# A two-layer GRU and a mixture of experts on one core: other places for small operations in five steps, and for two parts of the shared expert

## The chip, the core and the metric

The kernel runs on one of the eight cores of a Trainium2 chip. The metric is the device time of one execution in microseconds (us), as a median over several executions. A core has TensorE (PE, matrix products; PEld is its loading of weights), VectorE (DVE), ScalarE (ACT), GpSimd (POOL) and SyncE (SP). The first four compute; SP, ACT and POOL issue DMAs. [...]

## The reference

Two blocks with a residual around each. x is 2 x 1024 x 256, all in float32.

```
x = x + gru_block(x, cond)            # first block
x = x + moe_block(x, cond)            # second block

gru_block:  mixed = tanh(x @ W_in.T + b_in + cond)
            h1 = gru(mixed, layer 0);  h2 = gru(h1, layer 1)
            gate = sigmoid(cond @ W_gate.T + b_gate)
            return (gate * h2 + h2) @ W_out.T + b_out
  gru step: r, z = sigmoid(...);  n = tanh(xn + r * hn);  h = (1 - z) * n + z * h

moe_block:  shared = (silu(x @ w1) * (x @ w3)) @ w2          # 256 -> 512 -> 256
            s = sigmoid([x, cond] @ router_W)                # 8 experts
            the two best of s + bias; their s, normalised, are the shares
            routed = sum of share * (gelu(x @ W1e[e]) @ W2e[e])
            return (shared + routed) / 3
```

The recurrence runs over 1024 steps. The second block has 2048 tokens.

## The kernel before

**The recurrence in chunks.** The 1024 steps of a row are cut into 16 chunks of 62 steps (the first 32 steps are run once, in the run-up of the chunk that follows them). All chunks of both rows run side by side, as 32 columns of a state. A chunk does not know the state that it should begin with, so each layer first runs through the chunk before it (`AHEAD`: 62 steps for layer 0, 44 for layer 1), and takes the end as the beginning of the next (`go_round`). Whether the guess fits is measured at the end (`fit`), and a slow exact path exists for the case that it doesn't; it is not executed here, and its instructions follow a branch at the end.

**Ticks.** One loop runs over 126 ticks. In a tick layer 0 does one step and layer 1 does the step of two ticks earlier (`LAG`). `position(layer, tick)` is zero where the counted run of a layer begins: tick 62 for layer 0, tick 64 for layer 1. Layer 1 runs from tick 20 on. For each layer of a tick, `finish_scanned` issues: the sigmoid of both gates (ACT, L341), a scan for the sum inside tanh (DVE, L344), the tanh (ACT, L355), a product with the old state's row (DVE, L357), a scan that gives the new row (DVE, L360), and a transpose to the state that TensorE takes next (DVE, L369). TensorE then multiplies the state (`add_state`, L296) and the input of the next layer (`feed`, L268). VectorE takes the layers in turn.

The order is written out by hand: a scheduler is switched off for the loop (`manual_schedule`), and other work is put into named places of a tick: `place(tick, where, what)`, with "product" (TensorE, behind layer 0's state product), "behind" (TensorE, behind layer 1's), "n0" (before layer 0's tanh), "scan0" and "scan1" (on VectorE, between the product with the old row and the row's scan of layer 0 or 1) and "end". `plan` places the first block's output product for finished groups of tokens there; `front.prepare` places the gate of the first block: a product (`gate_sums`), its sigmoid, and what follows.

Three kinds of operation stand at the beginning of single steps. In the step at position -33 the state of the run-up that begins at step 0 must become zero: `keep` makes a masked row (`kept`, L337). At position 0 the state `begin` is turned back to rows by a transpose (`turned`, L484), called at the head of the tick. At tick 54 the gates' product stands in "product".

**The tail.** After the last tick `front.all_of` does the last group: its output product, the residual, the logits of the router (`route`, `keep_logits`) and the transposes to token rows. The results go to `given` in memory. The first part of the shared expert's hidden layer is begun in the last ticks (`begin_hidden`).

**The second block** (`moe`). Here a scheduler that knows the engines orders the instructions. There are 16 parts of the shared hidden layer (4 blocks of 512 tokens times 4 slices of 128); a part is four products of 512 columns (`hidden_sums`, L969), a sigmoid (L981), a silu (L982) and a product (L983). The routing is a chain of small VectorE operations from `raw` (L1083) to `pick` (L1179). After it, POOL gathers 128 tokens at a time for the experts (`fetch`, L1274), 35 blocks go through `go_through`, and their results go to `back`. `EARLY` parts are computed beside the routing, one (`FILL`) in the last expert blocks, and the rest in the last stage. There the order is again written by hand: POOL gathers the results back (`fetch_back`, L1335), eight at once and then two for every part; `behind` is a copy of one value (L1334) that makes POOL wait for a tile; `add_gone` adds the gathered rows (L1349); then for each of 16 tiles of tokens TensorE multiplies by w2 (L1367), VectorE adds (L1375) and ACT writes the tile out (L1376). The buffers for sigmoid and silu alternate between two.

Of the kernel before, what the change touches and what calls it, by code (L numbers as in the profile page):

```python
# [8 lines left out]
FP = mybir.dt.float32  # L9
# [8 lines left out]
P = 128  # L18
# [51 lines left out]

EARLY = 8
FILL = EARLY + 1
# [13 lines left out]
def gru_moe(ctx, tc, xT, vec, bias, w_in, wih0, whh0, wih1, whh1, w_out, w_gate, router, w1, w3, w2, w1e, w2e, out):  # L86
# [62 lines left out]
    class Steps:  # L149
# [177 lines left out]
        def finish_scanned(self, layer, to, tick, before_n, after_n, between, keep=None):  # L327
# [6 lines left out]
            sums = by_sum(ps)  # L334
            if keep is not None:
                kept = self.edge.tile([P, U], FP, name=f"kept{layer}")
                nc.vector.tensor_scalar(kept, h, keep, -1.0, ALU.mult, ALU.mult)  # L337
                h = kept

# [12 lines left out]

            n = self.step_pool.tile([P, U, 2], FP, name=f"n{layer}")
            before_n()
            nc.scalar.activation(n[:, :, 0], s[:, 1 : 2 * U : 2], AF.Tanh, scale=-1.0 if keep is None else keep)  # L355
# [45 lines left out]
    with ExitStack() as stack:  # L401
        g = Steps(stack, "", on_pe=False, rest_of_x=rest_of_x)
        g.gates = [
            [g.gru_only.tile([P, 2, U, 2], FP, name=f"gates{layer}{i}") for i in range(2)] for layer in range(2)
# [134 lines left out]
        def keep_of(layer, tick):  # L539

            return not_first[:, 0:1] if position(layer, tick) == -FIRST - 1 else None

        def let_wait(ins, copied):
# [52 lines left out]

        places = {}

        def place(tick, where, what):
            places.setdefault((tick, where), []).append(what)  # L600

        def placed(tick, where):
# [40 lines left out]
        place(last_tick - 1, "behind", lambda: begin_hidden("w3", [0]))  # L643
        place(last_tick - 1, "end", silu)
        for block in range(1, N // MB):
            place(block, "end", lambda block=block: spread(block))
# [4 lines left out]
        for i, todo in enumerate(front.prepare(g.bank)):  # L651
            for where, what in todo.items():
                place(AHEAD[0] - 8 + i, where, what)
        def negate_first():
# [31 lines left out]
        with tc.manual_schedule():  # L686
            for tick in range(AHEAD[0] + S + LAG):
                now = [layer for layer in range(2) if runs(layer, tick)]
                for layer in now:
                    if layer not in g.states:  # L690
                        g.states[layer], g.rows[layer] = zero_state, zero_row
                    elif position(layer, tick) == 0:
                        g.starts[layer] = g.states[layer] = begin[layer]
                        g.start_rows[layer] = g.rows[layer] = turned(g.starts[layer], f"start_row{layer}")
                work = work_of(tick)
# [74 lines left out]
    with tc.If(n_fit < P):  # L770
        with ExitStack() as stack:
# [45 lines left out]
            temp = [room[:, NT + i : NT + i + TB // D, :].rearrange("p s d -> p (s d)") for i in (0, TB // D)]  # L817
            front.hidden(0, 0, *(front.hidden_sums(g.bank, 0, 0, name)[0] for name in ("w1", "w3")), *temp)
        moe(tc, "_turn", front, out)


class Front:
# [17 lines left out]
    def prepare(self, bank):  # L840

        nc, vec_sb, later, ps = self.tc.nc, self.vec_sb, self.later, {}

        def gate_sums():
            ps["gate"] = bank("ps_gate")[:, 0 : KD * B].rearrange("p (k b) -> p k b", b=B)
            for m in range(KD):
                for k in range(KD):
                    last = nc.tensor.matmul(
                        out=ps["gate"][:, m, :],
                        lhsT=later["w_gate"][:, k, m * P : (m + 1) * P],  # L850
                        rhs=vec_sb[:, COND + k * B : COND + (k + 1) * B],
                        start=(k == 0),
                        stop=(k == KD - 1),
                    )
            return last
# [135 lines left out]

    def all_of(self, bank, group, between=lambda: None, behind=lambda: None):
        for m in range(KD):
# [5 lines left out]
        self.keep_logits(group)  # L999
        behind()  # L1000
        tiles = range(group * GS * R // P, (group + 1) * GS * R // P)
# [8 lines left out]
def moe(ctx, tc, tag, front, out):  # L1010
# [210 lines left out]

    parts = [(blk, m) for blk in range(N // TB) for m in range(KS)][1:]

# [104 lines left out]
    def fetch_back(behind=None):  # L1328
# [3 lines left out]
        yb = rows[:, AWAY + i % (ROWS - AWAY), :]  # L1332
        if behind is not None and i % 2 == 0:
            nc.gpsimd.tensor_copy(yb[0:1, 0:1], behind[0:1, 0:1])  # L1334
# [116 lines left out]
```

## Time and profile before

| what | value |
|---|---|
| time, median of 5 executions | 538.44 us (536.91 to 539.21) |
| the profiled execution | 539.21 us, of which the span from first to last instruction 537.5 us |
| PE busy | 512.7 us (95%), 7492 products |
| DVE busy | 385.7 us (72%) |
| ACT busy | 244.1 us (45%) |
| POOL busy | 76.9 us (14%) |
| HBM | 21.26 MB read, 9.57 MB written |
| from the last tick's end to the last instruction | 361 us to 537.5 us |

Lines of a profile are read like this. A group has its source line, engine, operation, what it writes and reads, the shape, a count, and then busy time, the mean of one in ns, and the idle time of the engine just before, with what ended it. A row of the timeline has its start and its length in us, and in brackets the idle time before it and what released it. "issue" means that the profile shows nothing that the engine waited for. TensorE's busy time is modelled: a matmul's end is not measured, and a full row does not mean that it works at its best. The granted clock is the share of TensorE's full clock that its throttle let through. "PE 512.7 (95%)" alone says little: what a change in one stage is worth is read from that stage.

### The profile page before, as it was taken

How to read it: one execution, taken by the hardware profiler on the slowest of the kernel's cores; microseconds unless marked ns; L12 is line 12 of the kernel's file. 1: busy time of each engine (PE TensorE's matmuls, PEld its weight loads, DVE VectorE, ACT ScalarE, POOL GpSimd, SP SyncE). 2: the span in 40 equal slices, each digit the busy share in tenths (PEclk: the TensorE clock that was granted, in tenths of full speed). 3: DMA queues.
4: the chain of work that ended last, by engine and by line, in shares of the span. 5: the costliest groups of instructions: out<-in, count | busy, mean ns of one | idle time of the engine just before them, and what ended most of it. 6: DMA issues, size and time to landing. Idle time of an engine off the chain costs nothing. (4 is left out here: it accounts for less than half of the span.)

```text
span 537.5 us, 18511 instructions
## 1 busy us (share of the span) xinstructions
PE 512.7 (95%) x7492; PEld 341.3 (64%) x7492; DVE 385.7 (72%) x1296; ACT 244.1 (45%) x833; POOL 76.9 (14%) x124
## 2 busy tenths in 40 slices
PE   7999999999999999999999999989999999999795
PEld 4556766676665545566665666654468888844584
DVE  3765699999888888888988888888943333335362
ACT  3444355665566555656566566632133333331000
POOL 1200000000000000000000000002064444037570
PEclk9999999999999999999999999999999999999888
DMA  8980000000000000000000000001034433223252
GB/s 287 372 256 2 2 3 4 3 4 2 4 32 3 12 1 4 2 23 22 4 22 8 17 23 3 22 22 60 1 97 124 124 119 128 70 70 98 88 168 85
DMA packets 23103, 32.13 MB, mean 60 GB/s; under 512 B 3056, under 2 KB 18544, under 8 KB 22992
## 3 DMA queue, kind: packets, MB, share of 16 engines
q1 hardware_dynamic: 17344, 19.94, 10.9%
q0 software_dynamic: 3216, 8.79, 5.8%
q10 hardware_dynamic: 2448, 2.11, 1.2%
q8 instruction: 63, 1.03, 0.8%
q14 instruction: 32, 0.26, 0.2%
HBM read 21.26 MB, written 9.57 MB: 57 GB/s over the span
## 5 line engine op out<-in xcount | busy, mean ns | idle before, releaser
L296 PE MATMUL ps_step<-whh_sb,h 128*32 128x192 f32 x3616 | 193.3, 331 | 5.2 <-DVE h L369 3.8
L296 PEld LDWEIGHTS ps_step<-whh_sb,h 128*32 128x32 f32 x3616 | 94.6, 109 | 71.3 <-DVE h L369 51.4
L360 DVE TENSOR_TENSOR_SCAN row<-gates,n 128x128 f32<-128x128 f32 x230 | 97.7, 425 | 29.6 <-ACT n L355 28.3
L344 DVE TENSOR_TENSOR_SCAN ps_step<-gates,ps_step 128x128 f32<-128x128 f32 x230 | 97.4, 424 | 14.3 <-ACT gates L341 14.2
L268 PE MATMUL ps_step<-wih_sb,h 128*32 128x192 f32 x1696 | 99.7, 328 | 4.1 <-ACT ps_step L526 2.4
L355 ACT ACTIVATE n<-ps_step 128x64 f32<-128x64 f32 x228 | 53.1, 233 | 111.0 <-DVE ps_step L344 110.9
L341 ACT ACTIVATE gates<-ps_step 128x128 f32<-128x128 f32 x230 | 66.8, 290 | 34.8 <-PE ps_step L296 25.7
L268 PEld LDWEIGHTS ps_step<-wih_sb,h 128*32 128x32 f32 x1696 | 57.5, 109 | 26.8 <-ACT ps_step L526 14.2
L369 DVE STREAM_TRANSPOSE h<-row 128x64 f32<-128x64 f32 x230 | 56.5, 246 | 8.1
L969 PE MATMUL ps_w<-x_sb,w_sb 128*128 128x512 f32 x128 | 57.3, 597 | 0.1
L268 PE MATMUL ps_in<-wih_sb,h 128*32 128x192 f32 x1024 | 54.4, 328 | 1.5 <-ACT h L257 1.1
L1239 DVE COPY hT<-ps_hT 128x256 f32<-128x256 f32 x35 | 14.9, 425 | 48.9 <-PE ps_hT L1237 47.1
L526 ACT COPY ps_step<-inputs 128x256 f32<-128x256 f32 x123 | 47.7, 388 | 0.0
L357 DVE SCALAR_TENSOR_TENSOR n<-gates,row 128x64 f32<-128x64 f32 x224 | 47.1, 210 | 0.0
L268 PEld LDWEIGHTS ps_in<-wih_sb,h 128*32 128x32 f32 x1024 | 34.1, 110 | 14.3 <-issue 4.6
L526 ACT COPY ps_step<-bt 128x256 f32<-128x256 f32 x106 | 39.9, 377 | 3.3
L1274 POOL DMA_INDIRECT inputs<-given,pick x35 | 33.3, 951 | 55.2 <-PE ps_xT L1237 31.8
L969 PEld LDWEIGHTS ps_w<-x_sb,w_sb 128*128 128x128 f32 x128 | 23.6, 190 | 27.1 <-issue 24.7
L1245 PE MATMUL ps_h<-w1e_sb,xT 128*128 x140 | 36.1, 380 | 0.7 <-DVE xT L1239 0.7
L1245 PE MATMUL ps_y<-w2e_sb,hT 128*128 x140 | 36.0, 380 | 0.0
L1335 POOL DMA_INDIRECT inputs<-back,slots x32 | 30.7, 959 | 29.8 <-issue 27.5
L1245 PEld LDWEIGHTS ps_y<-w2e_sb,hT 128*128 128x128 f32 x140 | 26.4, 190 | 4.8 <-DVE hT L1239 1.2
(179 smaller groups left out, 432.4 us busy)
## 6 DMA issues: line engine op xcount, KB each, us to landing
back<-y SPq DMA_DIRECT2D x35, 128.0 KB
w1e_sb<-in_w1e SPq DMA_DIRECT2D x1, 2048.0 KB
w2e_sb<-in_w2e SPq DMA_DIRECT2D x1, 2048.0 KB
given<-inputs SPq DMA_DIRECT2D x8, 256.0 KB
out_dram<-inputs ACTq DMA_DIRECT2D x16, 128.0 KB
whh_sb<-in_whh SPq DMA_DIRECT2D x2, 768.0 KB
x_sb<-in_xT SPq DMA_DIRECT2D x3, 512.0 KB
w_sb<-in_w SPq DMA_DIRECT2D x3, 512.0 KB
```

Source lines behind the costliest of these rows:

```text
L268: last = nc.tensor.matmul(out=out[cols(q), :, :], lhsT=given(k), rhs=self.wih[layer][:, k, q * 3 * U : (q + 1) * 3 * U].rearrange("p (g u) ...
L296: nc.tensor.matmul(out=by_sum(self.sums[layer])[cols(q), 0:3, :], lhsT=self.states[layer][:, k, :], rhs=self.whh[layer][:, k, q * 3 * U : ...
L341: nc.scalar.activation(gates[:, :, :, 1], sums[:, 1:3, :], AF.Sigmoid)
L344: nc.vector.tensor_tensor_scan(s, gates[:, 0, :, :].rearrange("p u i -> p (u i)"), ps[:, 0 : 6 * U : 3], 0.0, ALU.mult, ALU.add,)
L355: nc.scalar.activation(n[:, :, 0], s[:, 1 : 2 * U : 2], AF.Tanh, scale=-1.0 if keep is None else keep)
L357: nc.vector.scalar_tensor_tensor(n[:, :, 1], gates[:, 1, :, 1], 1.0, h, ALU.subtract, ALU.mult)
L360: nc.vector.tensor_tensor_scan(row.rearrange("p u i -> p (u i)"), gates[:, 1, :, :].rearrange("p u i -> p (u i)"), n.rearrange("p u i -> p ...
L369: nc.vector.transpose(to, row)
L526: return nc.scalar.copy(by_sum(banks[layer][tick % 2])[:, 0:4, :], g.sum_bias[1] if layer else inputs[:, group_of(0, tick), :, :],)
L969: last = self.tc.nc.tensor.matmul(out=ps, lhsT=self.later[name][:, k, m * P : (m + 1) * P], rhs=self.x1[:, k, blk * TB : (blk + 1) * TB], ...
L1245: nc.tensor.matmul(out=ps, lhsT=of[:, k, :], rhs=weights_sb[:, bass.ds(e * KD + k, 1), :], start=(k == 0), stop=(k == KD - 1),)
L1274: nc.gpsimd.indirect_dma_start(out=xg, out_offset=None, in_=given[:, :], in_offset=bass.IndirectOffsetOnAxis(ap=pick[:, i : i + 1], axis=0),)
```

## The change

Two groups of edits, in one kernel.

The first group shifts parts of the shared hidden layer. `EARLY` goes from 8 to 6 parts. The list of parts in `moe` begins with the third instead of the second, since a second part is computed in the tail: its first product stands between the output product and the routing's logits, and the rest behind the last transposes. The second half of the first part's w3 product moves to the last tick. Layer 1's `fit` moves behind the tail's `all_of`. In the last stage there are seven parts instead of six, and POOL copies a value ahead of every gather, not of every second.

The second group is about single ticks. The masked rows `kept` are made a half tick earlier, in "scan1" of tick 28 and "scan0" of tick 31. The gates' product is halved over two ticks, 53 and 54. The turn back to rows at positions 0 moves from the head of the tick to behind the sums' scan. The tanh keeps its scale from a tile in the masked steps.

```diff
-EARLY = 8
+EARLY = 6
@@ finish_scanned
-            if keep is not None:
-                kept = self.edge.tile([P, U], FP, name=f"kept{layer}")
-                nc.vector.tensor_scalar(kept, h, keep, -1.0, ALU.mult, ALU.mult)
-                h = kept
...
+            if h is self.turned_row.get(layer):
+                nc.vector.transpose(h, self.states[layer])
             before_n()
@@
+        def mask(layer):
+
+            kept = edge.tile([P, U], FP, name=f"kept{layer}")
+            nc.vector.tensor_scalar(kept, g.rows[layer], not_first[:, 0:1], -1.0, ALU.mult, ALU.mult)
+            g.rows[layer] = kept
...
+        place(AHEAD[0] - FIRST - 2, "scan1", lambda: mask(0))
+        place(AHEAD[0] + LAG - FIRST - 1, "scan0", lambda: mask(1))
@@
+        place(last_tick, "behind", lambda: begin_hidden("w3", [1]))
@@ front.prepare
-                place(AHEAD[0] - 8 + i, where, what)
+                place(AHEAD[0] - 9 + i, where, what)
...
-            {"product": gate_sums, "scan1": lambda: spread(0)},
-            {"n0": gates, "scan1": lambda: spread(1)},
+            {"product": lambda: gate_sums(0), "scan1": lambda: spread(0)},
+            {"product": lambda: gate_sums(1), "scan1": lambda: spread(1)},
+            {"n0": gates},
@@ position 0
-                        g.start_rows[layer] = g.rows[layer] = turned(g.starts[layer], f"start_row{layer}")
+                        g.start_rows[layer] = g.rows[layer] = g.turned_row[layer] = edge.tile(
+                            [P, U], FP, name=f"start_row{layer}"
+                        )
@@ the tail
-                    if position(layer, tick) == S - 1:
-                        fits.append(fit(layer))
+                    if layer == 0 and position(0, tick) == S - 1:
+                        fits.append(fit(0))
...
-            front.all_of(
-                g.bank,
-                GROUPS // GS - 1,
-                lambda: begin_hidden("w3", [1]),
-                lambda: nc.vector.tensor_tensor(
-                    front.hid(0, slice(0, TB)), begun["silu"], begun["w3"], ALU.mult
-                ),
+            nc.vector.tensor_tensor(front.hid(0, slice(0, TB)), begun["silu"], begun["w3"], ALU.mult)
+
+            def begin_next():
+                begun["next"], _ = front.hidden_sums(g.bank, 0, 1, "w1", None, [0])
+
+            front.all_of(g.bank, GROUPS // GS - 1, begin_next)
+            fits.append(fit(1))
+            front.hidden_sums(g.bank, 0, 1, "w1", begun["next"], [1])
+            pb, _ = front.hidden_sums(g.bank, 0, 1, "w3")
+            front.hidden(
+                0,
+                1,
+                begun["next"],
+                pb,
...
@@ moe
-    parts = [(blk, m) for blk in range(N // TB) for m in range(KS)][1:]
+    parts = [(blk, m) for blk in range(N // TB) for m in range(KS)][2:]
@@ fetch_back
-        if behind is not None and i % 2 == 0:
+        if behind is not None:
             nc.gpsimd.tensor_copy(yb[0:1, 0:1], behind[0:1, 0:1])
```

`gate_sums` takes the half `m` as an argument and is otherwise the same; `all_of` loses its argument `behind`; the exact path behind the branch computes two parts instead of one.

More of the change, by code (lines that the diff above doesn't have):

```diff
@@ L402, in gru_moe @@
         g = Steps(stack, "", on_pe=False, rest_of_x=rest_of_x)
+        g.turned_row = {}
         g.gates = [
@@ L541, in keep_of, with place @@
             return not_first[:, 0:1] if position(layer, tick) == -FIRST - 1 else None
+        places = {}
+        def place(tick, where, what):
+            places.setdefault((tick, where), []).append(what)
+        def mask(layer):
[4 more added lines that the diff above has]
+        place(AHEAD[0] + LAG - FIRST - 1, "scan0", lambda: mask(1))
         def let_wait(ins, copied):
@@ L592, in gru_moe @@
         next_rest()
-        places = {}
-        def place(tick, where, what):
-            places.setdefault((tick, where), []).append(what)
         def placed(tick, where):
@@ L744, in gru_moe @@
                 for layer in now:
-                    if position(layer, tick) == S - 1:
-                        fits.append(fit(layer))
+                    if layer == 0 and position(0, tick) == S - 1:
+                        fits.append(fit(0))
             for where in ("n0", "scan0", "end"):
                 placed(AHEAD[0] + S + LAG, where)
-            front.all_of(
-                g.bank,
-                GROUPS // GS - 1,
-                lambda: begin_hidden("w3", [1]),
-                lambda: nc.vector.tensor_tensor(
-                    front.hid(0, slice(0, TB)), begun["silu"], begun["w3"], ALU.mult
-                ),
+            nc.vector.tensor_tensor(front.hid(0, slice(0, TB)), begun["silu"], begun["w3"], ALU.mult)
[10 more added lines that the diff above has]
+                pb,
+                *(g.mixed_pool.tile([P, KD, MB], FP, name="mixed").rearrange("p k n -> p (k n)") for _ in range(2)),
             )
@@ L817, in gru_moe @@
             temp = [room[:, NT + i : NT + i + TB // D, :].rearrange("p s d -> p (s d)") for i in (0, TB // D)]
-            front.hidden(0, 0, *(front.hidden_sums(g.bank, 0, 0, name)[0] for name in ("w1", "w3")), *temp)
+            for m in range(2):
+                front.hidden(0, m, *(front.hidden_sums(g.bank, 0, m, name)[0] for name in ("w1", "w3")), *temp)
         moe(tc, "_turn", front, out)
@@ L842, in prepare, with gate_sums @@
         nc, vec_sb, later, ps = self.tc.nc, self.vec_sb, self.later, {}
[L844 to L854, printed above, removed]
+        def gate_sums(m):
+            if m == 0:
+                ps["gate"] = bank("ps_gate")[:, 0 : KD * B].rearrange("p (k b) -> p k b", b=B)
+            for k in range(KD):
+                last = nc.tensor.matmul(
+                    out=ps["gate"][:, m, :],
+                    lhsT=later["w_gate"][:, k, m * P : (m + 1) * P],
+                    rhs=vec_sb[:, COND + k * B : COND + (k + 1) * B],
+                    start=(k == 0),
+                    stop=(k == KD - 1),
+                )
             return last
@@ L990, in give, with all_of @@
         )
-    def all_of(self, bank, group, between=lambda: None, behind=lambda: None):
+    def all_of(self, bank, group, between=lambda: None):
         for m in range(KD):
@@ L999, in all_of @@
         self.keep_logits(group)
-        behind()
         tiles = range(group * GS * R // P, (group + 1) * GS * R // P)
```

## The prediction

> **What bounds the kernel now.** I read the busy time by stage first, then the chain that ended last, then the timeline around each place that the change touches. The stages (start:end, length; busy time of PE, PEld, DVE, ACT and POOL with counts; granted TensorE clock; DMA share and GB/s):
>
> ```profile
> 361.10:395.20 34.10, 33.22 (x139) 16.05 (x140) 29.36 (x88) 6.65 (x12) 7.68 (x29) 1.00 0.15 47
> 395.20:475.80 80.60, 79.79 (x429) 68.01 (x428) 28.04 (x73) 29.23 (x74) 28.34 (x30) 1.00 0.35 108
> 475.80:496.50 20.70, 20.68 (x49) 9.22 (x50) 11.05 (x19) 3.67 (x6) 14.98 (x19) 1.00 0.32 92
> 496.50:508.30 11.80, 8.00 (x35) 6.11 (x33) 3.14 (x6) 0.60 (x1) 7.07 (x10) 0.95 0.31 90
> 508.30:532.00 23.70, 23.54 (x95) 19.91 (x95) 14.89 (x36) 0.00 (x0) 11.32 (x15) 0.88 0.46 141
> ```
>
> From 361 on TensorE is full in every stage but one: 496.5 to 508.3, where 3.8 us are idle, and where the granted clock falls below 1. The chain says the same of the last 56 us:
>
> ```profile
> 475.82 20.84 PE ps_w L969 x48
> 496.66 6.48 PE ps_s L1367 x30
> ...
> 507.55 0.59 PE ps_s L1367
> 508.14 0.13 issue
> 508.27 23.59 PE ps_s L1367 x95
> 531.88 0.42 DVE inputs L1375
> ```
>
> Six parts of the shared expert (48 instructions in 20.84 us: 0.43 each, 3.43 to 3.47 a part), then 16 rows of output, each 8 instructions at 0.216 us, 1.73 together. From 496.49, 16 times 1.73 would end at 524.2; the last really ends at 531.85. So 7.6 us are lost. What that hole looks like in the timeline:
>
> ```profile
> 487.07 0.18 POOL L1334 COPY inputs<-sig 1x1 f32<-1x1 f32 x1
> 487.28 0.60 ACT L981 ACTIVATE sig<-ps_w 128x512 f32<-128x512 f32 x1 [5.43 <-POOL inputs L1334]
> 499.19 0.60 ACT L981 ACTIVATE sig<-ps_w 128x512 f32<-128x512 f32 x1 [5.95 <-PE ps_s L1367]
> 504.07 0.69 DVE L983 TENSOR_TENSOR inputs<-silu,ps_w 128x512 f32<-128x512 f32 x1 [3.56 <-remote]
> 508.33 0.42 DVE L1375 SCALAR_TENSOR_TENSOR inputs<-ps_s,inputs 128x256 f32<-128x256 f32 x1 [1.74 <-remote]
> ```
>
> Consumers of the sixth part and of output row 0 wait for TensorE until 499.19, 504.07 and 508.33, though its records have those products done at about 495, 497 and 498.6. No row tells what holds it. It falls in the time when POOL issues gathers without a pause (477.36 to 505.65), and ends 2.7 us after it.
>
> **The ticks.** From one transpose of layer 0's state to the next a plain tick takes 2.74 us, and VectorE's chain sets it. The touched ones take 2.95 and 2.93 (masks), 3.14 (gates' product), 3.09 and 3.24 (turns).
>
> ```profile
> 91.80 0.21 DVE L337 TENSOR_SCALAR kept<-row,not_first 128x64 f32<-128x64 f32 x1
> 160.53 1.05 PE L848 MATMUL ps_gate<-vec_sb,w_gate_sb 128*128 128x2 f32 x8
> 162.44 0.29 ACT L341 ACTIVATE gates<-ps_step 128x128 f32<-128x128 f32 x1 [0.48 <-PE ps_step L296]
> 183.56 0.20 DVE L484 STREAM_TRANSPOSE start_row<-begin 128x64 f32<-128x64 f32 x1
> ```
>
> - Masks: each pushes the next scan back by 0.12 (91.80 to 91.93, 98.85 to 98.97); that goes twice. The other 0.09 of those ticks stays: the tanh with its scale from a tile takes 0.32 instead of 0.23. The first mask's new place has 0.18 idle before the scan, as in a plain tick, and two copies of 0.29 together at 163.23 fit in that place without moving the scan (163.50): free. The second comes behind a 0.34 addition (L448) that already fills its place: I charge 0.12. Gain 0.12 (bounds 0 and 0.24).
> - Gates' product: 8 instructions hold TensorE 1.05, layer 1's state product comes late, and the gates wait 0.48; the tick is 0.40 longer. Halves of 0.53 end at 161.06, before layer 1's state is transposed (161.01) and its weights load (some 0.15 later). The nearest row is the context product, as many instructions as a half, in tick 60: the ticks there are 2.74 and 2.73. The half in tick 53 makes the next layer-1 input products move as one block, as in every tick with input work (2.74). Gain 0.40 (0.2 to 0.4). Copies on VectorE move a tick earlier into the same idle place.
> - Turns: they cost 0.12 (183.56 to 183.68) and 0.17 (189.48 to 189.65). In their new place the product with the row must wait for the whole transpose: 0.31 (scan) + 0.23 + 0.21 + 0.03 puts the row scan 0.78 behind the sums' scan, instead of 0.69. Gain 0.29 less 2 times 0.09: 0.11 (0 to 0.29).
>
> Together 0.63 less (0.2 to 0.93), all on the path.
>
> **The tail before routing.** The routing chain on VectorE starts with `raw`:
>
> ```profile
> 365.33 0.29 DVE L1083 TENSOR_TENSOR raw<-logits,context 128x128 f32<-128x128 f32 x1
> 387.83 0.20 DVE L1179 TENSOR_SCALAR pick<-few 128x39 int32<-128x39 f32 x1
> 388.32 1.18 POOL L1274 DMA_INDIRECT inputs<-given,pick x1 [19.99 <-DVE pick L1179]
> 395.19 0.60 PE L1237 MATMUL ps_xT<-ident,inputs 128*128 128x128 f32 x4
> ```
>
> In the changed kernel's order layer 1's fit (8 small operations, 1.2 us) and the whole second part (silu 0.69, product 0.68) stand ahead of `raw` on VectorE. That part's products on TensorE begin behind the last transposes at 365.0: half of w1 0.86, w3 1.72, last end 367.75; then product 0.68 and the count 0.11: `raw` at 368.5, 3.15 later. Fit, sigmoid (0.60) and silu end at 367.4 and are covered. From `raw` to `pick` both orders hold the same: 7 operations of parts on VectorE, 16, 22 and 8 instructions of parts on TensorE. So 22.5 us again, and `pick` at 391.0. Before, the first gather's packets ended at 391.95, the second's at 392.2, and TensorE came for them at 395.19 only, because 18 instructions of parts stood behind the last pick product. Now 2 stand there, done at 391.5. The first two gathers land at 395.1 and 395.35; the experts start at about 395.4. Two parts less in this stage buy nothing: 0.2 later (0 to 0.4). The w3 half that goes behind the last state product (1.02) fits in TensorE's idle 359.9 to 361.1: free; without that idle time it would cost its 1.02. It makes the last two transposed tiles of group 6, their copies on ScalarE and their write on SP (360.56) a microsecond later; they are due at the first gather, 391. On SP the write of zeros to `back` moves behind the read of the count; it is due at 476. Neither costs anything.
>
> **The last stage.** Six parts become seven: 8 times 0.43, 3.43 more on TensorE, on the chain. POOL copies a value before every gather instead of every second: a pair took 2.68 (487.07 to 489.75) and takes 2.82, as each copy's gather takes 1.41. POOL then ends its 32nd gather near 522, landing some 2.3 later; the row that needs it is computed after 526: covered. Each activation and silu of a part reuses the buffer of two parts before and so waits for POOL's copy of it; the last would run at 498.6 and 500.0, before TensorE's seventh part ends (500.2): covered, too, by 0.2.
>
> **Sum.** -0.63 + 0.2 + 3.43 = +3.0, with the hole unchanged. The profiled execution took 539.21 (span 537.5 and 1.7 around it), 0.77 above the median of the five; it would take 542.2, and the median 541.4. Bounds by those above: 540.5 to 542.5 for this case alone.
>
> **Rivals.**
> - *The hole closes* (the other side). One mechanism: if the dense gathers hold TensorE's completions, spacing them by copies frees it: 541.4 - 7.6 = 533.8. For it: the hole ends shortly after the run of gathers. Against: the run stays unbroken. Part 0's sigmoid is there at 477.8 but its copy comes at 487.07, for POOL is 9 us behind and gains 0.6 a part; so gathers go from one per 1.34 to one per 1.41 us. It decides from 3.0 us of the 7.6 on.
> - *The hole shrinks by about half*: 537.5 to 540, near no change. The same rows.
> - *A new idle time halves the clock.* TensorE would now wait from 391.5 to 395.3. In the hole, a gap of 4.6 us with two single matmuls in it was followed by matmuls 0.43 apart instead of 0.216, from 508.3 to 514: 3.0 us. If 3.8 empty us do the same: 544.4. Against: at 360 and 372 gaps of a microsecond did nothing, and nothing between is seen.
> - *The ticks don't shorten*: 542.0; inside the likeliest case's range.
>
> [...]
>
> **Chances.** Likeliest case 0.48 (540 to 543); hole closed 0.26; hole halved 0.12; clock halved 0.14. A difference under 0.3%, 1.6 us, can't be told from none here. Faster: 0.26 and a little of the halved hole, 0.28. Same: most of the halved hole and the lower edge of the likeliest, 0.12. Slower 0.60. The range from 533.5 to 544 leaves out a part of the closed hole and most of the halved clock, some 0.16.
>
> **What would show it.** Ticks 29, 32, 55, 62 and 64 at 2.83, 2.83 or 2.95, 2.74, 3.0 and 3.1. `raw` 3.15 later after the last tick, TensorE idle before the first xT for more than 3 us, 56 instead of 48 instructions of L969 in the last stage. I am wrong if output row 0's addition follows the seventh part's last matmul by 2 us instead of ten (the hole is closed), if `raw` doesn't move, or if TensorE's matmuls are 0.43 apart in the stage of the experts.

## The result, and the profile after

The changed kernel takes 539.22 us (median of 36 runs, 538.07 to 540.62), the kernel before 538.01 (61 runs, 534.71 to 539.33): a ratio of 1.0024, 95% interval 1.0017 to 1.0031. It is slower, as predicted, but by 1.2 us and not by 3.0. The profiled execution took 539.44, its span is 537.7; before it was 539.21 and 537.5.

So small a difference is a sum of large ones. The busy time by stage in the changed kernel (start:end, length; busy time of PE, PEld, DVE, ACT and POOL with counts; granted TensorE clock; DMA share and GB/s):

```profile
360.20:394.60 34.40, 29.15 (x133) 14.01 (x129) 29.08 (x88) 6.51 (x12) 5.79 (x27) 1.00 0.12 39
394.60:402.00 7.40, 6.57 (x20) 4.94 (x21) 2.12 (x5) 0.77 (x2) 5.05 (x6) 0.54 0.36 106
402.00:479.60 77.60, 76.17 (x410) 65.26 (x408) 26.19 (x67) 28.73 (x71) 25.17 (x27) 1.00 0.34 106
479.60:503.70 24.10, 24.10 (x57) 10.72 (x58) 12.20 (x21) 3.58 (x6) 18.93 (x28) 1.00 0.32 92
503.70:512.40 8.70, 8.58 (x40) 7.23 (x38) 3.65 (x7) 0.60 (x1) 5.92 (x10) 1.00 0.33 96
512.40:532.00 19.60, 19.45 (x89) 16.85 (x89) 13.72 (x34) 0.00 (x0) 11.65 (x18) 1.00 0.53 163
```

Two rows answer to the prediction. The experts now begin at a granted clock of 0.54, behind 3.73 us of idle time (`warm` below, with 0.25 us idle and a clock of 1.00, shows that the one makes the other). And from 503.70 on TensorE is full to the end: the hole is gone. The chain that ended last shows the same, with one pause of 0.16 where before 3.8 us lay idle:

```profile
494.85 9.01 PE ps_w L992 x21
503.86 8.42 PE ps_s L1389 x39
512.28 0.16 issue
512.44 19.46 PE ps_s L1389 x89
```

The timeline at the places that matter:

```profile
394.57 0.97 PE L1259 MATMUL ps_xT<-ident,inputs 128*128 128x128 f32 x4 [3.73 <-DMA inputs<-given,pick]
...
478.19 0.69 DVE L1006 TENSOR_TENSOR h<-silu,ps_w 128x512 f32<-128x512 f32 x1 [0.61 <-PE ps_w L992]
...
479.59 1.96 PE L992 MATMUL ps_w<-x_sb,w_sb 128*128 128x512 f32 x4 [1.43 <-DVEq L1342]
...
501.09 0.60 ACT L1004 ACTIVATE sig<-ps_w 128x512 f32<-128x512 f32 x1 [4.92 <-PE ps_w L992]
...
508.16 0.69 DVE L1006 TENSOR_TENSOR inputs<-silu,ps_w 128x512 f32<-128x512 f32 x1 [1.41 <-PE ps_s L1389]
...
512.42 0.42 DVE L1397 SCALAR_TENSOR_TENSOR inputs<-ps_s,inputs 128x256 f32<-128x256 f32 x1 [1.72 <-remote]
```

The first row is the 3.73 us of idle time. The second and third are a wait that the prediction does not have: the last stage's first product waits 1.43 us for VectorE behind the branch. Before, TensorE stood idle there for 0.15 us, and the load of that product's weights waited for ScalarE:

```profile
475.79 0.30 PEld L969 LDWEIGHTS ps_w<-x_sb,w_sb 128*128 128x128 f32 x2 [0.95 <-ACTq L1320]
```

The last three rows of the view after say that TensorE's completions, as I call the moments at which an engine that waits for a product goes on, are still late: row 0's product is done by its records near 505.4, its addition runs at 512.42. They no longer stop TensorE, though: its pause in the chain is 0.16 us.

To add this up I count from VectorE's first transpose (11.98 and 12.11 us into the span), since the start differs from one execution to the next, by 0.13 us between these two. The right-hand columns are the same two programs, profiled later (`before_again` and `after_again` below), in an execution without a hole:

| event | before | after | before_again | after_again |
|---|---|---|---|---|
| `raw` | 353.36 | 355.68 | 353.15 | 355.55 |
| `pick` | 375.85 | 378.08 | 375.65 | 377.94 |
| experts' first xT | 383.21 | 382.47 | 383.01 | 382.28 |
| last expert product begins | 461.60 | 463.96 | 461.26 | 462.69 |
| last stage's first part | 463.84 | 467.48 | 463.51 | 466.22 |
| output row 0 on TensorE | 484.52 | 491.59 | 484.18 | 490.32 |
| last products of the rows | 519.49 | 519.40 | 511.59 | 517.73 |
| end of the span | 525.51 | 525.60 | 517.37 | 523.65 |

From before to after, stage by stage: up to the experts -0.74, experts +3.10, branch +1.28 (2.24 to 3.52), parts +3.43 (20.68 to 24.11), rows -7.16 (34.97 to 27.81), end +0.18. Together +0.09.

### The profile page after: what moved, and what is told of

Read it like the earlier page. It is cut to its first block, busy times and chain, and to the rows that moved or that the text cites. A ratio compares the mean times of both kernels' runs of the same rounds, so it can differ in the third digit from the quotient of the medians.

```text
span 537.7 us, 18535 instructions
## 1 busy us (share of the span) xinstructions
PE 511.9 (95%) x7492; PEld 341.7 (64%) x7492; DVE 385.9 (72%) x1296; ACT 243.7 (45%) x833; POOL 80.4 (15%) x136
## 5 line engine op out<-in xcount | busy, mean ns | idle before, releaser
L268 PE MATMUL ps_step<-wih_sb,h 128*32 128x192 f32 x1696 | 98.6, 328 | 4.0 <-ACT ps_step L525 2.7
L1267 PE MATMUL ps_h<-w1e_sb,xT 128*128 x140 | 38.3, 399 | 0.8 <-PE ps_xT L1259 0.8
L1357 POOL DMA_INDIRECT inputs<-back,slots x32 | 31.8, 994 | 29.3 <-issue 27.6
L1307 ACT ACTIVATE he<-ps_h 128x256 f32<-128x256 f32 x35 | 13.4, 383 | 40.1 <-PE ps_h L1267 33.9
```

The lines of the kernel that those rows point to most:

```text
L268: last = nc.tensor.matmul(out=out[cols(q), :, :], lhsT=given(k), rhs=self.wih[layer][:, k, q * 3 * U : (q + 1) * 3 * U].rearrange("p (g u) ...
L1267: nc.tensor.matmul(out=ps, lhsT=of[:, k, :], rhs=weights_sb[:, bass.ds(e * KD + k, 1), :], start=(k == 0), stop=(k == KD - 1),)
```

## Experiments

Every kernel ran beside the kernel before on the same chip, and the ratios are to that. One thing has to be told first. The kernel before took 531.56, 531.29 and 531.66 us beside the first three groups of runs below (chips numbered 13, 15 and 7), and 537.86, 537.56 and 537.48 beside the last three (15, 5 and 2). The second kind is like the result's 538.01. Nothing differs in the programs, and number 15 is in both. I call them runs without and with the hole, since the profiles differ in that.

### Is the hole the program's?

Both kernels once more, unchanged.

> The kernel before, unchanged, profiled beside the other three. In the four runs so far TensorE's completions were 1.72 us apart through the whole last stage, though POOL gathered without a pause, and the kernel before took 531.6 there instead of 538. Theory E (the hole is a property of the chip or of the moment and not of the program): where the time is about 531.6, output row 0's addition comes at about 499 instead of 508.3 and the last row's at 525, and the granted clock is 1.0 from 480 to 530; where it is about 538, the completions arrive late again. Theory P (the hole is the program's, and the four kernels closed it each in its own way): late completions and a 7 us hole whatever the time of the others.

> The changed kernel, unchanged, timed beside the kernel before. Theory E: without a hole to close, the change costs what its own steps cost: ticks -0.6, half clock at the experts' start +2 to +3, wait for VectorE behind the branch +1.3, seventh part +3.4, together +6 to +7, ratio 1.012; where the kernel before has its hole, +1.3 as in the result, ratio 1.002. Theory P: +1.3 everywhere.

Measured: before_again 530.56 (one run; the kernel before beside it 531.29), after_again 539.33, ratio 1.0148 (1.0134 to 1.0162). The chain of before_again over the last 48 us, and its first output row:

```profile
474.89 20.84 PE ps_w L969 x48
495.73 27.64 PE ps_s L1367 x128
```
```profile
498.22 0.42 DVE L1375 SCALAR_TENSOR_TENSOR inputs<-ps_s,inputs 128x256 f32<-128x256 f32 x1
```

Row 0's addition runs at 498.22 instead of 508.33, the 16 rows take 27.64 without a pause. In after_again (by stage, columns as above) the rows take the same 27.70, and what the change costs is plain:

```profile
394.63:402.00 7.37, 6.66 (x25) 5.24 (x26) 2.03 (x5) 1.14 (x3) 5.67 (x6) 0.65 0.33 106
402.00:475.40 73.40, 73.40 (x402) 63.79 (x401) 24.79 (x65) 26.36 (x69) 24.56 (x26) 1.00 0.35 110
475.40:478.60 3.20, 1.77 (x6) 0.50 (x4) 1.38 (x2) 1.99 (x3) 0.00 (x0) 1.00 0.13 44
478.60:502.70 24.10, 24.10 (x57) 10.71 (x58) 13.37 (x23) 4.18 (x7) 18.97 (x28) 1.00 0.30 91
502.70:530.40 27.70, 27.70 (x129) 24.10 (x127) 16.48 (x38) 0.00 (x0) 17.20 (x28) 1.00 0.47 146
```

From the table: up to the experts -0.73, experts +2.16, branch +1.28, parts +3.43, rows 0, end +0.14, together +6.28, and 0.97 more lie ahead of the first transpose: the two profiled executions differ by 7.2. The medians differ by 8.0, since after_again's profiled execution, 537.73, was the fastest of its five. So theory P falls: the same program has the hole in some executions and not in others. The changed kernel takes 539.2 and 539.3 in both, because its rows lose next to nothing to the hole (27.81 us with it, 27.41 without); the kernel before takes 538 or 531.

### The idle time ahead of the experts, and the wait behind the branch

`warm` fills the idle place with products that nobody reads, one part's worth; `half_filled` (one product) fills half of it. Both take one more of the seven banks, as the program calls its tiles for TensorE's results (`p_any`), which it hands on from product to product.

```diff
     shared_hidden(parts[:EARLY])
+    idle = bank("ps_w1")                                  # warm
+    for _ in range(2):
+        front.hidden_sums(bank, 0, 2, "w1", idle)
...
+    front.hidden_sums(bank, 0, 2, "w1")                   # half_filled, instead
```

> The changed kernel, with one part's worth of products that nobody reads (the first product of a part, twice, 3.44 us) behind the last part before the experts, where TensorE stood idle 3.73 us. Everything else stays: two parts before the ticks' end, six beside the routing, seven in the last stage. Theory H (the idle time halves the clock, and that costs 3.1 us in the experts): granted clock 1.0 in the stage of the experts, their end 3.1 us earlier less the 0.3 by which the filling is too long, time 536.4. Rival (the slow products after the idle time are hidden behind the gathers of the experts or are caught up later): time 539.2 to 539.6.

> The changed kernel with one product of a part (1.72 us, nobody reads it) behind the last part before the experts. It does two things: it leaves some 1.9 us of TensorE's idle time in place of 3.7, and it takes one bank, so that the last stage's first product finds a bank that ScalarE read last and not VectorE. Theory H: an idle time of 1.9 us does not halve the clock: experts in 78.9 instead of 80.4 to 81.5 us. Theory B (the 1.3 us behind the branch come from the bank that the rotation hands to the first product): the last stage's first product starts 1.1 to 1.4 us sooner after the experts' end. Both: 535.5 to 536.2 where the changed kernel takes 539.3. If only the bank counts, 538; if only the clock, 536.5 to 537.3; if neither, 539.3.

Measured: warm 536.23, ratio 1.0088 (1.0075 to 1.0101); half_filled 536.62, ratio 1.0093 (1.0079 to 1.0107); both without the hole, where the changed kernel has 1.0148. Of warm, the first transposes of the experts and the stage that begins with them:

```profile
394.55 0.91 PE L1262 MATMUL ps_xT<-ident,inputs 128*128 128x128 f32 x4 [0.25 <-DMA inputs<-given,pick]
```
```profile
394.55:402.00 7.45, 6.36 (x35) 5.28 (x36) 2.79 (x7) 1.52 (x4) 5.67 (x6) 1.00 0.36 106
```

The idle time is 0.25 instead of 3.73, the clock 1.00 instead of 0.54 to 0.65, 35 products run in the window instead of 20 to 25. The experts take 78.86 us from first xT to last product, against 81.49 in the result's profile and 80.41 in after_again. The last stage still begins 3.53 us after the last expert product. So theory H holds: the idle time costs through the clock, 2.6 us against the one profile and 1.6 against the other, in which by the granted clock of the experts' first stage (0.65 over 7.37 us, against 0.54 over 7.40) only some 5.2 us of the halved clock fell upon the experts instead of 6.8. The medians of warm and after_again differ by 3.1.

Of half_filled, the first xT, the last stage's first product with the load of its weights, and the first stage; then that product of warm:

```profile
394.82 0.95 PE L1260 MATMUL ps_xT<-ident,inputs 128*128 128x128 f32 x4 [1.97 <-DMA inputs<-given,pick]
...
477.47 0.30 PEld L992 LDWEIGHTS ps_w<-x_sb,w_sb 128*128 128x128 f32 x2 [0.95 <-ACTq L1343]
477.50 0.67 PE L992 MATMUL ps_w<-x_sb,w_sb 128*128 128x512 f32 x1
```
```profile
394.82:402.00 7.18, 6.04 (x24) 4.75 (x25) 2.03 (x5) 0.93 (x3) 5.52 (x6) 0.76 0.33 104
```
```profile
476.93 8.39 PE L992 MATMUL ps_w<-x_sb,w_sb 128*128 128x512 f32 x19 [1.43 <-DVEq L1345]
```

Theory B's number is met: the first product begins 2.25 us after the last expert product begins instead of 3.52, and waits for ScalarE again. So the 1.28 us are no fixed price of the branch or of the seventh part. But that they come from the bank, as theory B has it, is not shown: warm takes one bank more as well, and its first product still waits for VectorE and begins after 3.53. The wait of 3.52 to 3.53 stands in the changed kernel, after_even, parts and warm; all others have 2.24 to 2.25. What decides between the two stays open. The wait for VectorE is long because VectorE reaches the branch only behind the `FILL` part's last product (478.19, 0.69 long).

Theory H's number falls: 1.97 us of idle time, with a wait of 1.00 behind the first transposes, still halved the clock, for 3.41 us instead of 6.83 (0.76 over 7.18 us), and the experts took 80.43. The time, 536.62, lies where theory H alone was expected to put it, though the profile shows theory B's gain: by the profiles half_filled saves 1.1 us against after_again, by the medians 2.7.

### One part back beside the routing

`early7` puts a real part into the idle place, and the last stage has six parts again. `early7_even` has also the copies of the kernel before.

```diff
-EARLY = 6
+EARLY = 7
...
-        if behind is not None:
+        if behind is not None and i % 2 == 0:              # early7_even only
```

> The changed kernel with EARLY = 7: the seventh part is really computed in that idle place, and the last stage has six parts again, with a copy before every gather. The idle time, the half clock and one part's 3.43 us in the last stage all go. Theory L (TensorE's completions arrive late while POOL gathers without a pause, and this costs time only where TensorE is so far ahead that it runs out of banks): with six parts it is ahead again, the hole of 7 us returns, output row 0's addition comes about 2 us after the last gather of the unbroken run (near 507), time 537.4. Theory C (a copy before every gather is what closed the hole): no hole, 16 rows end near 524, time 531.

> As the kernel with EARLY = 7, but a copy before every second gather only, as in the kernel before: the kernel before with the tick edits and the second part's other place, and nothing of the last stage changed. Theory L: the run of gathers ends 1 to 1.5 us earlier than with all copies, the hole is there, time 536.5 to 537.4. Theory C: the hole is there too, 537.4, so that the difference to the kernel with all copies is 6 to 7 us and not under 1.

Measured, without the hole: early7 534.72, ratio 1.0063 (1.0050 to 1.0075); early7_even 531.80, ratio 1.0004 (0.9995 to 1.0012). Both theories' numbers are missed, since there was no hole to keep or close. What differs between the two is the copies alone, and they cost 2.9 us: the last gather begins at 509.58 instead of 506.70 us after the first transpose, and the end of early7 hangs on gathers and no more on TensorE:

```profile
524.09 1.07 DVE L1371 SCALAR_TENSOR_TENSOR inputs<-inputs,share 128x256 f32<-128x256 f32 x2 [1.23 <-DMA inputs<-back,slots]
525.07 0.75 DVE L1397 SCALAR_TENSOR_TENSOR inputs<-ps_s,inputs 128x256 f32<-128x256 f32 x2
```

So with six parts the copies are not covered. And early7_even says what the second part's other place is worth together with the ticks: nothing that can be measured.

### The ticks

`parts` is the changed kernel without the edits of ticks; `ticks` the kernel before with them; `mask_gate` the kernel before with the masks and the gates' product, the turns left in place. The edits are those of the diff above.

```diff
# parts: of the changed kernel, undone
-        place(AHEAD[0] - FIRST - 2, "scan1", lambda: mask(0))
-        place(AHEAD[0] + LAG - FIRST - 1, "scan0", lambda: mask(1))
...
-            {"product": lambda: gate_sums(0), "scan1": lambda: spread(0)},
-            {"product": lambda: gate_sums(1), "scan1": lambda: spread(1)},
+            {"product": lambda: (gate_sums(0), gate_sums(1))[1], "scan1": lambda: spread(0)},
...
-            if h is self.turned_row.get(layer):
-                nc.vector.transpose(h, self.states[layer])
```

> The changed kernel with the masks, the gates' product and the turns as in the kernel before: the part's edits alone. The ticks' edits are worth 0.5 to 0.6 by the trace (last transpose of layer 0 at 354.66 instead of 355.19), so the time should be 0.5 above the changed kernel's, 539.7, and 1.7 above the kernel before. Rival: the shift moves where the gathers and the halved clock fall, and the difference is anything else.

> The kernel before with the edits of single ticks alone: masks, gates' product in halves, turns behind the sums' scan. From the two traces: masks 0.13 less between ticks 28 and 34, gates 0.40 less between 53 and 56, turns 0.08 more between 61 and 67. Time 0.4 to 0.6 below the kernel before, ratio 0.999. Rival: an earlier start of the gathers or the experts is lost again behind them, ratio 1.000.

> The kernel before with two of the tick edits alone: the masked rows made a half tick earlier and the gates' product in halves; the turns stay where they were. By the traces so far the masks are worth 0.13, the gates 0.40, and the turns cost 0.08 to 0.1: 0.5 below the kernel before, and 0.1 below the kernel with all three, ratio 0.999. Rival: none of it arrives at the end, ratio 1.000.

> The kernel before with the masks and the gates' product alone, a second time: 0.5 below the kernel before on any chip, if what the ticks save arrives at the end; ratio 0.9984 to 0.9995. Where the kernel before has its hole, the saving could also vanish in it: 1.000.

Measured: parts 538.71, ratio 1.0139 (1.0122 to 1.0155); ticks 531.05, ratio 0.9997 (0.9988 to 1.0006); mask_gate 530.88, ratio 0.9984 (0.9974 to 0.9994); these without the hole. With the hole, mask_gate_2 538.37, ratio 1.0011 (0.9995 to 1.0028).

Parts tells nothing: it should lie 0.5 above the changed kernel, and at 1.0139 and 1.0148 (in another group) the two can't be told apart; what the halved clock costs varies by more than that (the experts take 81.49 us in the result's profile and 80.41 in after_again). Mask_gate is faster than the kernel before where there is no hole, by 0.8 us; with the turns on top (ticks) no gain can be told from none. With the hole nothing of it can be seen. Of mask_gate_2, the stage of the hole:

```profile
495.90:507.70 11.80, 8.43 (x36) 6.65 (x35) 3.14 (x6) 0.60 (x1) 7.25 (x10) 0.93 0.29 90
```
```profile
507.74 0.42 DVE L1382 SCALAR_TENSOR_TENSOR inputs<-ps_s,inputs 128x256 f32<-128x256 f32 x1 [2.43 <-remote]
```

It is the hole of the kernel before, 3.4 us idle in 11.8, and the saving of the ticks can't be seen behind it.

### What holds TensorE's completions

Two edits of the kernel before, and one of the changed kernel. `plain` takes the gathers away: transfers of as many rows in order, issued by SP (which rows are added is left out of the computation). `copies` puts a copy before every gather. `after_even` is the changed kernel with a copy before every second only.

```diff
-        nc.gpsimd.indirect_dma_start(                      # plain
-            out=yb,
...
+        nc.sync.dma_start(out=yb, in_=back[i * P : (i + 1) * P, :])
...
-        if behind is not None and i % 2 == 0:              # copies; after_even is the reverse
+        if behind is not None:
```

> The kernel before, with the 32 gathers of the last stage replaced by plain transfers of as many rows in order, issued by SP: which rows are added is left out, and POOL issues nothing there but its copies. Where the kernel before takes 531: TensorE's completions stay 1.72 apart, rows end when TensorE ends, about 523.4, time 530 to 531.5, so the gathers cost nothing there. Where the kernel before takes 538: theory G (the gathers' building or their semaphores hold the completions) gives 530 to 532, and a hole all the same (538) would clear the gathers.

> The kernel before with a copy before every gather instead of every second, and nothing else. If there is no hole: POOL needs 1.44 instead of 1.34 us a gather, the gathers end 2.4 later and the last rows wait for them, as in the kernel with EARLY = 7: +2.7 to +3, ratio 1.005. If there is a hole (before at 538): theory C, the copies close it, 531 to 534; theory L, it stays, 538 to 540.

> The kernel before with plain transfers by SP in place of the last stage's gathers (which rows are added is left out), a second time, for the case that the kernel before takes 538 beside it: then 530 to 532 would say that the gathers hold TensorE's completions, and 538 that they do not. Where the kernel before takes 531, it takes 531 as well.

> The kernel before with a copy before every gather, a second time, for the case that the kernel before takes 538 beside it: theory C 531 to 534, theory L 538 to 541. Where it takes 531: 535 again, ratio 1.007.

> The changed kernel with a copy before every second gather, as in the kernel before: only the last stage's copies are undone. Where the kernel before takes 531: with seven parts the gathers are not late even with all copies, so the time is the changed kernel's, 538 to 539.3, ratio 1.013 to 1.015. Where the kernel before takes 538: theory C (copies closed the hole) 541 to 545; theory L (TensorE being 7 us further behind keeps it from running out of banks) 538.5 to 539.5.

Measured without the hole: plain 531.01 (one run; the kernel before 531.66), copies 535.00, ratio 1.0070 (1.0056 to 1.0084): there the gathers cost nothing, and twelve copies more cost 3.7 us, as the late gathers did in early7. Measured with the hole (the kernel before 537.86): plain_2 531.45 (one run), copies_2 536.29, ratio 0.9975 (0.9957 to 0.9992), after_even 538.78, ratio 1.0033 (1.0016 to 1.0049).

Plain_2 beside a kernel with the hole: row 0's addition and the stage of the rows.

```profile
499.30 0.42 DVE L1370 SCALAR_TENSOR_TENSOR inputs<-ps_s,inputs 128x256 f32<-128x256 f32 x1
```
```profile
496.80:524.40 27.60, 27.60 (x129) 23.99 (x127) 17.41 (x40) 0.00 (x0) 1.84 (x5) 1.00 0.44 140
```

The rows take 27.60 and nothing is late: without POOL's gathers there is no hole, and as many bytes come all the same. It is one execution, so its neighbours alone don't say that it had a hole to lose. Its trace does: between 400 and 460 us, in the stage of the experts, whose gathers it keeps, it holds 696 records of landed transfers, where plain holds 1008. In the same way the profiles with the hole hold 617 to 650 there and the others with gathers 864 to 911. So theory G holds in that the gathers make the hole; whether by their building or by their semaphores, no run shows. Copies_2 shows that their density counts; row 0's addition is still late (503.01, where copies had it at 499.74), but TensorE goes on:

```profile
503.01 0.42 DVE L1375 SCALAR_TENSOR_TENSOR inputs<-ps_s,inputs 128x256 f32<-128x256 f32 x1 [1.75 <-PE ps_s L1367]
```
```profile
496.80:524.80 28.00, 27.92 (x129) 23.89 (x127) 17.02 (x39) 0.00 (x0) 21.21 (x34) 1.00 0.49 145
```

27.92 of 28.00 busy: theory C is right about TensorE. It gains only 1.6 of 6.4 us because the late gathers then set the end. After_even shows that a second way leads to the same: without the copies, but with a last stage that reaches its rows later, the rows take 27.70 and there is no stall either. So the copies alone would have closed the hole for TensorE, and the rest of the change alone as well.

### Which gathers

The kernel of mask_gate, with copies before the 12 gathers beside the parts: in `parts_copies` the gathers beside the rows keep theirs at every second, in `parts_only` they have none.

```diff
-        if behind is not None and i % 2 == 0:
+        if behind is not None and (i % 2 == 0 or i < BACK + 12):   # parts_copies
...
+        if behind is not None and BACK <= i < BACK + 12:           # parts_only
```

> The kernel before with the masks and the gates' product, and a copy before every gather that stands beside a part (12 gathers, 6 copies more), while the gathers beside the rows keep a copy before every second. Six copies at 0.1 to 0.19 put the last gather 0.6 to 1.2 later than in the kernel before instead of 2.3. Where the kernel before takes 531: 530.9 to 532, ratio 0.9985 to 1.001. Where it takes 538: if the spacing in the stretch 485 to 500 is what keeps TensorE's completions moving, no stall of TensorE, rows in 27.4 to 28, time 532 to 535; if the stretch beside the rows counts, 536.5 to 538.5.

> The same, and no copies at all before the gathers beside the rows: 12 copies in all as in the kernel before, but all of them beside the parts. The last gather comes as early as in the kernel before or earlier. Where the kernel before takes 531: 530.5 to 531, ratio 0.998 to 1.000. Where it takes 538: 531 to 534 if spacing beside the parts is enough; 537 to 541 if the unbroken gathers beside the rows hold the completions then.

> The kernel with the masks, the gates' product and the copies beside the parts once more, for the case that the kernel before takes 531 beside it (it took 537.6 beside the first): then the six copies more put the last gather 0.6 to 1.2 later, the tick edits save 0.5 to 0.8, and if the last rows wait for the gathers as with all copies (3.2 at the end for 2.3 of the gathers), 531.5 to 532.5, ratio 1.000 to 1.002. Where it takes 538: 535.6 again.

All three met the hole. Parts_copies: 535.61 beside 537.56, ratio 0.9947 (0.9928 to 0.9967), and a second time 535.88 beside 537.48, ratio 0.9959 (0.9944 to 0.9975). Parts_only: 544.88, ratio 1.0134 (1.0112 to 1.0156), above the 541 that was the most expected. The rows of parts_copies take 29.57 us, 2.2 more than without a hole, and its time lies between what was expected of each stretch. Of parts_only, the additions of rows 2 and 3, POOL's last gather, and the stage between:

```profile
510.24 0.42 DVE L1382 SCALAR_TENSOR_TENSOR inputs<-ps_s,inputs 128x256 f32<-128x256 f32 x1 [2.24 <-remote]
520.07 0.42 DVE L1382 SCALAR_TENSOR_TENSOR inputs<-ps_s,inputs 128x256 f32<-128x256 f32 x1 [8.44 <-remote]
```
```profile
519.13 0.95 POOL L1342 DMA_INDIRECT inputs<-back,slots  x1 [0.30 <-issue]
```
```profile
507.00:520.00 13.00, 5.97 (x17) 3.03 (x15) 2.26 (x6) 0.00 (x0) 9.95 (x11) 0.81 0.42 126
```

From 505 to 519 the gathers follow each other by 1.25 us (once 1.47) with no copy between, and for that time hardly a completion of TensorE arrives; the next addition is there one microsecond after the last gather begins. TensorE is busy 5.97 of 13 us. This is the clearest run: taking copies away where they stood made the hole larger, by 9 us against parts_copies, though its last gather came 3.0 us earlier. Parts_copies is faster than the kernel before where there is a hole, and the changed kernel is slower. Where there is none, no run shows what it does; there mask_gate is ahead of the kernel before, at 0.9984.

## Why the prediction was wrong

The direction was right, the size was not: +3.0 forecast, +1.2 measured. That the direction came out was luck: the three terms that the sum did not have, +3.1, +1.3 and -7.2, come to -2.8, just short of turning it. Where the kernel before has no hole, the same change costs 8.0. Its steps:

- **Ticks, -0.63.** Right: from the first transpose of layer 0's state to the last it is 342.31 instead of 342.97, -0.66. By parts: masks (ticks 28 to 34) -0.14, predicted -0.12; gates (53 to 56) -0.40, predicted -0.40; turns (61 to 67) +0.08, predicted -0.11. That makes -0.46; the other -0.20 lies in ticks that no edit touches, and the same program differs by as much from one execution to the next (342.97 in before, 342.77 in before_again). So the sum was met in part by chance. The turns' term was mis-sized in one place. The row scan stands 0.92 behind the sums' scan, and not 0.78:

```profile
183.12 0.43 DVE L340 TENSOR_TENSOR_SCAN ps_step<-gates,ps_step 128x128 f32<-128x128 f32 x1
183.46 0.22 DVE L351 STREAM_TRANSPOSE start_row<-begin 128x64 f32<-128x64 f32 x1
183.71 0.23 DVE L355 SCALAR_TENSOR_TENSOR n<-gates,start_row 128x64 f32<-128x64 f32 x1
183.86 0.16 DVE L914 COPY context<-ps_context 128x8 f32<-128x8 f32 x1
184.04 0.42 DVE L358 TENSOR_TENSOR_SCAN row<-gates,n 128x128 f32<-128x128 f32 x1
```

  The same 0.92 stands at layer 1's turn (190.41 to 191.33). The 0.23 more than in a plain tick is larger than the transpose's own 0.12 to 0.17 at the head of the tick.
- **The tail: `raw` 3.15 later, the experts 0.2 later.** Right: `raw` came 2.32 later, which is 2.98 behind the ticks; `pick` followed it by 22.40 us, before by 22.49; the experts began 0.08 earlier behind the ticks. Two parts fewer before them bought nothing, and TensorE stood idle for 3.73 us where 3.8 were predicted.
- **That idle time costs nothing.** Wrong. It stood among the rivals, with a chance of 0.14 and a price of 3.0. The experts took 3.1 longer in the result's profile and 2.2 in after_again; of that warm takes 2.6 and 1.6 back. The 0.5 that is left (78.86 instead of 78.38) is not the clock's: early7 and early7_even have it too (78.81 and 78.86), at a clock of 1.00 there; its cause is open. The argument against the rival, that gaps of a microsecond did nothing, says nothing of 3.8 us: half_filled shows the clock halved after 1.97 us and a wait of 1.00.
- **The last stage, +3.43.** Right for the parts (20.68 to 24.11). What was missing is the wait ahead of them: 1.28 us, because the first product now waits for VectorE behind the branch and not for ScalarE. The prediction went through the instructions that were added and moved, and not through what the first product behind the branch waits for. What turned that wait is open: one more product ahead of the experts turned it back in half_filled, two on one bank in warm did not.
- **POOL's copies are covered.** Right with seven parts (after_even 1.0033, the changed kernel 1.0024), wrong with six (copies 1.0070). The last gather began at 526.15, not near 522, and was still in time.
- **"With the hole unchanged".** Wrong, and the largest step: -7.16. The rival had the right mechanism: dense gathers hold the completions, and copies between them let these through (row 0's addition at 499.30 in plain_2, 503.01 in copies_2 and 508.33 in the kernel before; 9.8 us without an addition in parts_only). It was set down because a gather in 1.41 us instead of 1.34 looked too small a change. But the change also moved TensorE back against POOL's run of gathers: row 0 begins 23.84 us after the first gather instead of 19.13, that is 3.43 for the seventh part and 1.28 for the wait, and after_even shows that this would have done without the copies. A stall that arises from one engine being ahead of another can't be kept as a constant when the change moves one of the two. The sign that was to tell a closed hole misled as well: row 0's addition came 8.6 us behind the seventh part, nearer to the ten of an open hole than to the two of a closed one, and TensorE ran through all the same.

With the terms as measured, -0.7 + 3.1 + 1.3 + 3.4 - 7.2 + 0.2 gives +0.1 in the profiled spans, beside +1.2 in the medians: the profiled execution before lay 1.2 above its median, the one after 0.2. Two rivals came true together and worked against each other.

Still open: why the same program has the hole in some executions and not in others. The runs only show that it goes with the gathers where it is there.

## What to carry to other kernels

A loss that depends on how two engines stand to each other is not a term that stays as it is: when a change delays one by several microseconds, ask first whether the loss is still there, and run the kernel before at another time or place to see whether it is the program's at all. Take away work ahead of a wait only after asking what the engine does in the time it wins: here two parts less gave TensorE 3.7 us of idle time, then a halved clock (0.54 over 7.40 us), and the work itself came back later at full price. And when work is taken away or added ahead of a branch, look at which engine the first product behind it waits for: here it changed from ScalarE to VectorE and cost 1.3 us where no instruction had been added.

## What the runs showed of the hardware

- **The clock.** In the result's profile TensorE's clock was halved for 6.83 us after 3.73 us of idle time, and for as long in the kernel before, from 507.16 on, in its hole; in half_filled for 3.41 us after 1.97 (0.76 over 7.18 us), in parts_only for 13.65 us from a stage on with 7 us idle of 13 (0.81 over these 13 us, 0.78 over the 20 behind them). These are two, one and four times 3.41. In the kernel before no idle time ahead of the fall was that long: there were 0.92 us, 1.02 us and a third that had lasted 1.33 us when the clock fell; in half_filled the longest was 1.97 us. In the 3.41 us ahead of the fall TensorE's records fill 0.75 us in the kernel before and 0.55 us in the result's profile.
- **Completions and gathers.** Where the hole appears, TensorE's completions arrive late in the stretches of the last stage in which POOL issues gathers back to back, every 1.25 to 1.5 us, and the fewer pauses there are between them the later: row 0's addition came at 499.30 without gathers (plain_2), at 503.01 with a copy before each (copies_2), at 507.74 with a copy before every second (mask_gate_2). With no copies at all beside the rows, no addition ran for 9.8 us (parts_only). Where the hole does not appear, the same gathers delay nothing (498.22 in before_again).
- **Records.** In the profiles with the hole the trace holds 1618 to 1718 records of transfers' completions, in those without it 2415 to 2418 for the same transfers; plain_2, without the gathers of the last stage, has 2051, and plain 2418. So where completions are late, many are also not recorded one by one. The records thin out from the experts' first gathers on, long before the hole (630 in before between 400 and 460 us, 869 in before_again), while up to 350 us the counts agree (482 in before). Whether both have one cause is not shown. Every run on record has a recorded span and clock, so none shows whether the hole would be there without recording.
